# A two-layer graph attention kernel: transposes by 64-row halves, column products by 64x64 tiles, maps in the score tile

## The chip, the cores and the metric

The kernel runs on one NeuronCore of a Trainium2 chip. The core has five engines with queues of their own: TensorE (PE; its weight loads are listed apart as PEld), VectorE (DVE), ScalarE (ACT), GpSimd (POOL) and SyncE (SP), which here only starts transfers. TensorE writes its results to PSUM, where VectorE and ScalarE read them; a tile there has two banks of 512 fp32 numbers on each of 128 partitions. The metric is the device time of one execution in microseconds (us). Before the change it is 1046.4 us, the median of 14 runs (1036.08 to 1050.53).

## What is computed

Eight graphs of 2048 nodes with 64 features share one adjacency matrix. A first attention layer has four heads; keys, queries and values are all the projected nodes `h`. A second layer has one head, and two layer norms follow.

```python
def _gat_layer(h, mask, b):
    scores = jnp.einsum('...nd,...md->...nm', h, h)
    scores = jnp.where(mask, scores, NEG)
    attn = jax.nn.softmax(scores, axis=-1)
    return jnp.einsum('...nm,...md->...nd', attn, h) + b
...
    mask = graph + jnp.eye(N, dtype=graph.dtype) > 0
    h = jnp.einsum('bnc,hdc->bhnd', x, Wh)
    out_h = _gat_layer(h, mask[None, None], bh[None, :, None, :])
    cat = jnp.transpose(out_h, (0, 2, 1, 3)).reshape(B, N, H * D)
    z = jax.nn.leaky_relu(cat, negative_slope=0.2)
    h2 = jnp.einsum('bnk,dk->bnd', z, Wo)
    out2 = _gat_layer(h2, mask[None], bo)
    z2 = jax.nn.leaky_relu(out2, negative_slope=0.2)
    ...
    out = (z2 - mu) * jax.lax.rsqrt(var + LN_EPS) * gamma + beta
    return out
x = _layernorm(x + _L0_gnn_ref(x, adj, ...), axis=-1)
```

The adjacency is sparse, and denser towards the first nodes: the chance of an edge falls with the indices of both its ends.

## The kernel before

The kernel does not compute all 2048 by 2048 scores. The first 56 nodes ("hub") attend to all nodes. The other 1992 are dealt into 166 sets of 12 nodes. For each set the kernel makes a list of at most 128 nodes that any of the 12 is linked to, and works on these alone. A row of the tables in memory holds one node of all eight graphs: four pairs of graphs (index `q`, Q = 4), each pair 128 features (`p` = 0 or 1 within it) with a one on either side for the sums.

The order on every engine's queue is the order in which the code calls the operations. Waits between engines are put in by the framework, tile by tile. A PSUM tile with one buffer is written anew only when all its readers are done, and accesses of two engines to one bank are kept apart.

**Hub stage** (0 to about 150 us). The adjacency is loaded and packed, the lists of the first sets are picked on VectorE (max and match_replace), `turn_x` (L580) transposes the nodes into `xT`, and the hub's scores and values are made.

**Layer one, the sets** (about 156 to 620 us). Two sets make a group, 83 groups (NG). The loop at L1017 is pipelined: in round `i` it works on several groups at different steps. In the order of the code, TensorE does

- scores of group i+1 (`scores`, L814): 32 products of 64x64 tiles over 48 columns into tile `s` (tag S), each in two passes for fp32, so 64 in the profile. Row halves are the two graphs of a pair, and each writes its own bank;
- project of group i-1 (L525): 8 products of 64x64 over 96 columns into tile `cat` (tag C);
- values of group i (L837): 16 products of 128x64 over 65 columns into `o` (tag O);
- maps of group i-2 (`second_maps`, L873): 4 products of 128x64 over 96 columns, into columns 384 to 479 of the first bank of `cat`;
- rows of group i-3 (`second_rows`, L889): one transpose of 128x96 into the second bank of `cat`;
- columns of group i+4 (`columns`, L802): 2 products of 128x128 over 192 columns into both banks of `cat`. Their stationary operand `gram` holds a 64x64 matrix for each head twice, on its diagonal blocks, with zeros in the other two;
- the first turn of group i+3 (`turn`, L509): 4 transposes of 128x128 of gathered rows into the first bank of `t` (tag T);
- the turned values of group i (`turn_values`, L859): 4 transposes of 112x128 into `o`;
- the second turn of group i+3: 4 transposes into the second bank of `t`.

VectorE takes the mask from the scores (`weigh`, L824), inverts the sums and scales the values (`invert`, L848: two reciprocals and a product into `osb`), applies the leaky slope (`leak`), copies the maps (`keep_own`, L882, into `own`), adds the bias to the rows (`keep_rows`, L892, into `rowt`) and in the rounds that have them picks more lists (`some`). ScalarE adds the head bias (`leaky`, L514), copies the turned rows to `xTg` (L1030), takes the exponential (`lift`, L831), copies the columns to `y` (`keep_columns`, L808) and the turned values to `otb` (`keep_values`, L865). GpSimd starts the gathers of group i+5 (`gather`, L790: two indirect transfers into a ring of ten row tiles), gathers the sets' own nodes (`own_rows`, L795, every second round), copies `own`, and in the early rounds packs adjacency pieces (`more`). SP stores the rows of `keep_rows` to `table2`, and from round 30 moves the nodes for the last norm.

**Layer two** (about 625 to 1040 us). Four sets make a step, 42 steps. `turn2` (L1314) transposes the gathered rows of four sets with `turn`, 16 transposes into two `t2` tiles, which ScalarE copies to `xTg` (L1320). `scores2` (L1126) reads these as its moving operand. ScalarE's exponential, transposes of the scores (`turn_scores`, L1140), VectorE's masking (`keep_scores`, L1147, into `es`), `values2` (L1157) and the norms follow.

The names that the change touches: `turn` and its three callers (`turn_x`, the loop, `turn2`); `own_rows`, `columns` and `keep_columns`; `scores` and `scores2`, which read what was turned; `values`, `invert`, `turned`, `turn_values`, `keep_values`; `second_rows` and `keep_rows`; and the loop itself.

## Time and profile before

| | before |
|---|---|
| median of 14 runs | 1046.4 us |
| profiled execution, its own time | 1045.82 us |
| span in the profile, first to last instruction | 1043.9 us |
| mean granted TensorE clock | 0.924 |
| TensorE busy | 80% of the span |
| VectorE, ScalarE, GpSimd busy | 59%, 50%, 44% |
| transposes of layer-one and layer-two rows (L512) | 1328, 201.1 us busy |
| column products (L806) | 320, 65.4 us busy |
| turned values (L863) | 332, 45.9 us busy |
| transposes of rows for table2 (L890) | 83, 26.6 us busy |

"Busy" counts the time in which at least one instruction of the group runs. Records of TensorE overlap, since its instructions are pipelined: the mean length of one L512 is 284 ns, but four that follow each other take 0.44 us from the first to the start of what comes next. The chain of work that ended last is followed back from the last instruction: at each step to what released it, or to the instruction before it on its engine. Idle time is put down to the instruction whose end came last among those waited for. fp32 products are listed in two passes, so the counts of plain products are twice the code's; transposes run in one.

### The profile page before, as it was taken

The page shows a single profiled execution, that of the slowest core. Times are in us where ns is not written, and L with a number is a line of the kernel's source. Part 1 is how long each engine was busy: PE and PEld are TensorE (multiplying, and loading weights), DVE is VectorE, ACT ScalarE, POOL GpSimd, SP SyncE. Part 2 cuts the span into 40 slices and gives each one's busy share as a digit, 9 for nine tenths or more (in the row PEclk, how much of TensorE's full clock was granted, in tenths as well). Part 3 has the DMA queues.
Part 4 walks back from the last instruction along what each step waited for, and adds up shares of the span by engine and source line. Part 5 has one row for each costly group of instructions (what it writes and reads, how often), then busy time and mean ns, then how long its engine had stood idle before and what let it go on. Part 6 is the DMA issues. An engine that isn't in the chain of part 4 may idle for free.

```text
span 1043.9 us, 42066 instructions
## 1 busy us (share of the span) xinstructions
PE 838.6 (80%) x18437; PEld 706.5 (68%) x18437; DVE 613.3 (59%) x1369; ACT 517.5 (50%) x961; POOL 462.2 (44%) x612
## 2 busy tenths in 40 slices
PE   2976778899999999999999983677787777778740
PEld 2654567778899888888888963466666656666640
DVE  3359735688777777555555553024455555556695
ACT  2323335455666666666666651344444454545541
POOL 5542224463444556555565505344434353535400
PEclk9999889999999999999999995699889898989975
DMA  8885413453444555555555406455555565556521
GB/s 176 236 233 149 139 35 106 135 134 94 105 115 115 144 154 147 156 145 157 157 150 154 125 24 175 134 158 141 147 154 161 152 173 158 155 157 160 163 59 32
DMA packets 81794, 145.22 MB, mean 139 GB/s; under 512 B 30146, under 2 KB 46466, under 8 KB 81602
## 3 DMA queue, kind: packets, MB, share of 16 engines
q0 software_dynamic: 26720, 88.55, 31.7%
q1 hardware_dynamic: 37842, 49.65, 16.4%
q10 hardware_dynamic: 17040, 4.25, 2.2%
q8 instruction: 147, 2.41, 1.0%
q14 instruction: 45, 0.37, 0.1%
HBM read 123.91 MB, written 18.48 MB: 136 GB/s over the span
## 4 chain that ended last, share of the span: by engine, by line
PE 68%; DVE 10%; issue 7%; ACT 6%; DMA 4%; another core or an unknown queue 3%; POOL 1%; SPq 0%; ACTq 0%; DVEq 0%; POOLq 0%
PE t L512 15%; PE s L821 10%; PE o L846 8%; PE cat L806 5%; PE s L1133 5%; PE o L1165 3%; PE cat L531 3%; PE o L863 3%; PE cat L880 3%; ACT xTg L1320 3%; PE sh L1277 2%; PE e L1144 2%; PE cat L890 2%; PE oh L608 1%
## 5 line engine op out<-in xcount | busy, mean ns | idle before, releaser
L792 POOL DMA_INDIRECT g<-table,index x332 | 329.4, 992 | 411.0 <-PE o L846 173.7
L512 PE MATMUL t<-ident,g 128*128 128x128 f32 x1328 | 201.1, 284 | 24.4 <-DMA g<-table,index 12.3
L512 PEld LDWEIGHTS t<-ident,g 128*128 128x128 f32 x1328 | 160.8, 146 | 41.9 <-issue 33.8
L1320 ACT COPY xTg<-t 128x1024 f32<-128x1024 f32 x83 | 80.4, 1015 | 133.5 <-PE t L512 89.2
L826 DVE TENSOR_TENSOR e<-s,mask 128x768 f32<-128x768 f32 x83 | 79.5, 957 | 105.0 <-PE s L821 104.6
L821 PE MATMUL s<-y,xTg 64*64 64x48 f32 x5312 | 114.9, 222 | 5.2 <-issue 4.7
L821 PEld LDWEIGHTS s<-y,xTg 64*64 64x64 f32 x5312 | 98.6, 134 | 25.1 <-issue 16.4
L1152 DVE TENSOR_TENSOR es<-e,linked 128x384 f32<-128x384 f32 (+1 forms) x42 | 23.1, 551 | 141.3 <-PE t L512 94.3
L518 ACT ACTIVATE z<-cat,bhp 128x192 f32<-128x192 f32 x166 | 60.7, 417 | 85.6 <-PE cat L531 85.6
L846 PE MATMUL o<-g,e 128*64 128x65 f32 x2656 | 97.4, 227 | 0.0
L846 PEld LDWEIGHTS o<-g,e 128*64 128x64 f32 x2656 | 85.7, 140 | 9.9 <-issue 0.2
L1133 PE MATMUL s<-xTg,bd 128*32 128x128 f32 x1328 | 66.0, 314 | 29.6 <-issue 21.1
L1030 ACT COPY xTg<-t 128x1024 f32<-128x1024 f32 x83 | 84.0, 1012 | 1.9 <-PE t L512 1.9
L833 ACT ACTIVATE e<-e,shifts 128x768 f32<-128x768 f32 x83 | 79.2, 954 | 2.1 <-DVE e L826 2.0
L1133 PEld LDWEIGHTS s<-xTg,bd 128*32 128x32 f32 x1328 | 43.7, 124 | 47.6 <-issue 39.8
L812 ACT COPY y<-cat 128x384 f32<-128x384 f32 (+1 forms) x80 | 40.7, 508 | 66.2 <-DVE rowt L894 46.3
L597 ACT ACTIVATE e<-e,shifts 128x896 f32<-128x896 f32 x32 | 33.4, 1042 | 77.8 <-DVE e L594 68.4
L806 PE MATMUL cat<-xo,gram 128*128 128x192 f32 (+1 forms) x320 | 65.4, 327 | 0.0
L680 POOL TENSOR_SCALAR a<-raw 120x1024 bf16<-120x1024 int32 (+1 forms) x34 | 38.1, 1124 | 58.4 <-DMA raw<-in_adj_dram 32.6
L1165 PE MATMUL o<-g,es 128*32 128x65 f32 x2656 | 57.2, 242 | 7.1 <-DVE y_s L1188 5.1
L853 DVE RECIPROCAL rall<-o 64x8 f32<-64x8 f32 x166 | 34.1, 205 | 45.2 <-PE o L846 43.7
L854 DVE TENSOR_TENSOR osb<-o,rall 128x512 f32<-128x512 f32 x83 | 57.4, 691 | 2.9
(177 smaller groups left out, 1449.3 us busy)
## 6 DMA issues: line engine op xcount, KB each, us to landing
raw<-in_adj_dram SPq DMA_DIRECT2D x32, 480.0 KB
table<-xb SPq DMA_DIRECT2D x22, 256.0 KB
xr_s<-table SPq DMA_DIRECT2D x21, 256.0 KB
g<-table,index POOLq DMA_INDIRECT x332
table<-x SPq DMA_DIRECT2D x16, 260.0 KB
x<-in_x_dram ACTq DMA_DIRECT2D x32, 128.0 KB
table<-rowt SPq DMA_DIRECT2D x166, 24.4 KB
xb<-in_x_dram SPq DMA_DIRECT2D x164, 24.0 KB
```

Source lines behind the costliest of these rows:

```text
L512: nc.tensor.transpose(tp[:, q * P:(q + 1) * P], rows[:, q, 1:1 + P], ident)
L518: nc.scalar.activation(z[:, hp], cat[:, :, hp * n:(hp + 1) * n], AF.Identity, bias=bhp[:, hp:hp + 1], scale=1.0)
L792: nc.gpsimd.indirect_dma_start(out=t.rearrange("n q c -> n (q c)"), out_offset=None, in_=table, in_offset=bass.IndirectOffsetOnAxis(ap=ind ...
L806: nc.tensor.matmul(cat[:, k, 2 * GM:2 * GM + n], gram[:, g % 2 * 2 + k, :], held["x", g // 2][:, :n], start=True, stop=True)
L821: nc.tensor.matmul(sp[half(r), p, (q * 2 + j) * M:(q * 2 + j + 1) * M], xt[half(p), j, q, half(r)], y[half(p), (j * Q + q) * M:(j * Q + q ...
L826: nc.vector.tensor_tensor(e[:, :16 * M].rearrange("p (a q n) -> p a q n", a=2, q=Q), sp[:, :, :8 * M].rearrange("p a (q n) -> p a q n", q= ...
L833: nc.scalar.activation(e[:, :16 * M], e[:, :16 * M], AF.Exp, bias=shifts[:, 0:1], scale=1.0)
L846: nc.tensor.matmul(op[half(p), j, o0:o0 + K1], e[:, c0:c0 + 64], rw[j][:, q, sums(p)], start=True, stop=True)
L1030: nc.scalar.copy(t, held.pop(("tp", i + 2)))
L1133: nc.tensor.matmul(sp[q * 32:(q + 1) * 32, k, :], bd[u % 3][:, k, q, :], xt[:, s % 2, q, :], start=True, stop=True, tile_position=(0, q * 32))
L1165: nc.tensor.matmul(op[t * 32:(t + 1) * 32, f, k * W2 + p:k * W2 + p + K1], e[:, 2 * q + p, k, :], rw[:, q, sums(p)], start=(a == 0 and k = ...
L1320: nc.scalar.copy(t, tp)
```

## The change

Transposes are split by rows. `turn` makes two transposes for each 128x128 block: rows 0 to 63 into the first bank of the tile, rows 64 to 127 into the second, with 64 columns each. A group's second set (`j` = 1) goes beside the first within each bank. `turned_rows` gives readers the view (bank, set, pair, column). `turn_values` and `second_rows` are split in the same way, and `invert` lays its result out so that each half has its 48 rows together.

The columns are four 64x64 products for each head, two row halves by two column halves, so that the zero blocks of `gram` are not used. Each row half writes one bank, and both column halves. For this the operand `xo` has its second half with the two partition halves exchanged: `own_rows` makes three copies for one. `keep_columns` and `scores` read the result accordingly.

The maps go to columns 384 to 479 of the score tile `s` and no longer to `cat`; the rows stay in `cat`, 64 columns in each bank. In the loop the copy to `xTg` stands ahead of project; maps, columns, rows and their copies stand right behind the gathers, ahead of `leak`, the adjacency pieces and the picks; the copy of the columns stands ahead of those of maps and rows; and both turns come ahead of the turned values. One job of the hub (`slow.pop`) moves to the head of the round. In `scores2` the moving operand has two pieces of 64 columns.

```diff
@@ -508,6 +508,12 @@
-    def turn(tp, rows):
+    def turn(tp, rows, j=0):
         for q in range(Q):
-            nc.tensor.transpose(tp[:, q * P:(q + 1) * P], rows[:, q, 1:1 + P], ident)
+            c0 = (j * Q + q) * 64
+            for r in range(2):
+                nc.tensor.transpose(tp[:, r, c0:c0 + 64], rows[half(r), q, 1:1 + P], ident[half(r), half(r)])
+    def turned_rows(t):
+        return t.rearrange("c r (j q n) -> c r j q n", j=2, q=Q)
@@ -581,4 +587,5 @@
         tp = two(f"px{i}")
-        turn(tp[:, 0, :], xrow[i])
-        nc.scalar.copy(xT[:, :, i * P:(i + 1) * P], tp[:, 0, :].rearrange("c (q n) -> c q n", q=Q))
+        turn(tp, xrow[i])
+        nc.scalar.copy(xT[:, :, i * P:(i + 1) * P].rearrange("c q (r n) -> c r q n", r=2),
+                       tp[:, :, :Q * 64].rearrange("c r (q n) -> c r q n", q=Q))
@@ -796,6 +803,9 @@
-        w = min(4, NS - 4 * m)
         t = held["x", m] = work.tile([P, 2 * GM], F32, tag="xo", name=f"xo{m}", bufs=2)
-        src = xT[:, :, HUB:].rearrange("c q (k s) -> c s q k", s=NS)[:, 4 * m:4 * m + w]
-        nc.gpsimd.tensor_copy(t[:, :w * 48].rearrange("c (s q k) -> c s q k", s=w, q=Q), src)
+        v = t.rearrange("c (b s q k) -> c b s q k", b=2, s=2, q=Q)
+        src = xT[:, :, HUB:].rearrange("c q (k s) -> c s q k", s=NS)
+        nc.gpsimd.tensor_copy(v[:, 0], src[:, 4 * m:4 * m + 2])
+        b0 = min(4 * m + 2, NS - 2)
+        for r in range(2):
+            nc.gpsimd.tensor_copy(v[half(r), 1], src[half(1 - r), b0:b0 + 2])
@@ -803,15 +813,19 @@
-        n = min(4, NS - 4 * (g // 2)) * 48
+        t = held["x", g // 2]
         for k in range(2):
-            nc.tensor.matmul(cat[:, k, 2 * GM:2 * GM + n], gram[:, g % 2 * 2 + k, :], held["x", g // 2][:, :n], start=True, stop=True)
+            for r in range(2):
+                for p in range(2):
+                    nc.tensor.matmul(cat[half(p), r, (2 + k) * GM:(3 + k) * GM], gram[half(r), g % 2 * 2 + k, half(r)],
+                                     t[half(r), (p ^ r) * GM:((p ^ r) + 1) * GM], start=True, stop=True)
     def keep_columns(g, cat):
-        n = min(4, NS - 4 * (g // 2)) * 48
         if g % 2 == 0:
             held["y", g // 2] = work.tile([P, 2 * GM, H], F32, tag="yg", name=f"y{g // 2}", bufs=2)
-        nc.scalar.copy(held["y", g // 2][:, :n, g % 2 * 2:g % 2 * 2 + 2], cat[:, :, 2 * GM:2 * GM + n].rearrange("p a n -> p n a"))
+        h0 = g % 2 * 2
+        nc.scalar.copy(held["y", g // 2].rearrange("p (b n) h -> p b h n", b=2)[:, :, h0:h0 + 2, :],
+                       cat[:, :, 2 * GM:4 * GM].rearrange("p b (k n) -> p b k n", k=2))
     def scores(g, sp):
-        xt = held.pop(("T", 1, g)).rearrange("c j (q n) -> c j q n", q=Q)
-        y = held["y", g // 2][:, g % 2 * GM:(g % 2 + 1) * GM, :].rearrange("p n h -> p (n h)")
+        xt = turned_rows(held.pop(("T", 1, g)))
+        y = held["y", g // 2].rearrange("p n h -> p (n h)")
         for j in range(2):
@@ -819,5 +833,6 @@
                 for p in range(2):
+                    c0 = ((g % 2) ^ p) * GM * H + (j * Q + q) * M
                     for r in range(2):
-                        nc.tensor.matmul(sp[half(r), p, (q * 2 + j) * M:(q * 2 + j + 1) * M], xt[half(p), j, q, half(r)],
-                                         y[half(p), (j * Q + q) * M:(j * Q + q + 1) * M], start=True, stop=True)
+                        nc.tensor.matmul(sp[half(r), p, (q * 2 + j) * M:(q * 2 + j + 1) * M], xt[half(p), r, j, q, :],
+                                         y[half(p), c0:c0 + M], start=True, stop=True)
@@ -834,3 +849,3 @@
-    OQ = 256
+    OW = D + 2
@@ -843,3 +858,3 @@
                     c0 = (p * 8 + q * 2 + j) * M
-                    o0 = q // 2 * OQ + q % 2 * (D + 2) + p
+                    o0 = q * OW + p
@@ -848,11 +863,11 @@
     def invert(g, op):
-        v = op.rearrange("a j (k c) -> a (j k) c", k=2)[:, :, :2 * (D + 2)].rearrange("a w (s c) -> a w s c", s=2)
-        osb = held["o", g] = work.tile([P, 4, 2, D], F32, tag="osb", name=f"osb{g}")
-        r = rall[:, g, :].rearrange("a (w s) -> a w s", w=4)
+        v = op[:, :, :Q * OW].rearrange("a j (q c) -> a j q c", q=Q)
+        osb = held["o", g] = work.tile([P, 2, Q, D], F32, tag="osb", name=f"osb{g}")
+        r = rall[:, g, :].rearrange("a (j q) -> a j q", j=2)
         for p in range(2):
             nc.vector.reciprocal(r[half(p)], v[half(p), :, :, p * K1])
-        nc.vector.tensor_tensor(osb, v[:, :, :, 1:K1], r.unsqueeze(3).to_broadcast([P, 4, 2, D]), OP.mult)
+        nc.vector.tensor_tensor(osb, v[:, :, :, 1:K1], r.unsqueeze(3).to_broadcast([P, 2, Q, D]), OP.mult)
     def turned(op):
-        return op.rearrange("a j (k c) -> a (j k) c", k=2)[:, :, 2 * (D + 2):2 * (D + 2) + 112]
+        return op[:, :, Q * OW:Q * OW + 4 * M]
@@ -860,5 +875,8 @@
-        osb = held.pop(("o", g))
+        osb = held.pop(("o", g)).rearrange("a j q c -> a (j q c)")
         for w in range(4):
-            nc.tensor.transpose(turned(op)[:, w, :], osb[:112, w].rearrange("a s c -> a (s c)"), ident[:112, :112])
+            for p in range(2):
+                mine = slice(p * 64, p * 64 + M)
+                nc.tensor.transpose(turned(op)[:, p, w * M:(w + 1) * M], osb[mine, w * P:(w + 1) * P],
+                                    ident[mine, mine])
@@ -867,6 +885,3 @@
         ot = held["ot", g] = work.tile([P, H, GM], F32, tag="ot", name=f"otb{g}")
-        v = turned(op)
-        for p in range(2):
-            nc.scalar.copy(ot.rearrange("c h (p w n) -> c p h w n", p=2, w=4)[:, p],
-                           v[:, :, p * 64:p * 64 + M].rearrange("c w (n h) -> c h w n", h=H))
+        nc.scalar.copy(ot.rearrange("c h (p m) -> c p m h", p=2), turned(op).rearrange("c p (m h) -> c p m h", h=H))
@@ -889,3 +904,5 @@
     def second_rows(g, pr):
-        nc.tensor.transpose(pr, held.pop(("own", g)), ident)
+        t = held.pop(("own", g))
+        for r in range(2):
+            nc.tensor.transpose(pr[:, r, :], t[half(r)], ident[half(r), half(r)])
@@ -893,3 +910,3 @@
         r = rowts[g % 4]
-        nc.vector.tensor_tensor(r[:GM, 1:1 + P], pr, bob[:GM].rearrange("n p d -> n (p d)"), OP.add)
+        nc.vector.tensor_tensor(r[:GM, 1:1 + P].rearrange("n (p d) -> n p d", p=2), pr, bob[:GM], OP.add)
         dst = table2[HUB:, :].rearrange("(n s) (q c) -> s q n c", s=NS, q=Q)
@@ -1017,8 +1034,11 @@
     for i in range(-4, NG + 3):
+        if i >= 1 and slow and len(slow) % 3:
+            slow.pop(0)()
+        sp = one(f"s{i + 1}", "S")
         if 0 <= i + 1 < NG:
-            sp = one(f"s{i + 1}", "S")
             scores(i + 1, sp)
             weigh(i + 1, sp)
-        if i >= 1 and slow and len(slow) % 3:
-            slow.pop(0)()
+        if 0 <= i + 2 < NG:
+            t = held["T", 1, i + 2] = work.tile([P, 2, 512], F32, tag="xTg", name=f"xTg{i + 2}", bufs=3)
+            nc.scalar.copy(t, held.pop(("tp", i + 2)))
         cat = one(f"cat{i}", "C")
@@ -1027,5 +1047,2 @@
             held["z", i - 1] = leaky(cat, GM, f"z{i - 1}")
-        if 0 <= i + 2 < NG:
-            t = held["T", 1, i + 2] = work.tile([P, 2, 512], F32, tag="xTg", name=f"xTg{i + 2}", bufs=3)
-            nc.scalar.copy(t, held.pop(("tp", i + 2)))
         if 0 <= i + 1 < NG:
@@ -1043,2 +1060,14 @@
             (add_beta if i % 2 else load_own)((i - 30) // 2)
+        if 0 <= i - 2 < NG:
+            second_maps(i - 2, sp[:, 0, 384:384 + GM])
+        if 0 <= i + 4 < NG + NG % 2:
+            columns(i + 4, cat)
+        if 0 <= i - 3 < NG:
+            second_rows(i - 3, cat[:GM, :, 384:448])
+        if 0 <= i + 4 < NG + NG % 2:
+            keep_columns(i + 4, cat)
+        if 0 <= i - 2 < NG:
+            keep_own(i - 2, sp[:, 0, 384:384 + GM])
+        if 0 <= i - 3 < NG:
+            keep_rows(i - 3, cat[:GM, :, 384:448])
         if 0 <= i - 1 < NG:
@@ -1059,13 +1088,2 @@
             assert i + 1 + LOOK >= NG or 2 * (i + 1 + LOOK) + 1 < ready
-        if 0 <= i - 2 < NG:
-            second_maps(i - 2, cat[:, 0, 384:384 + GM])
-        if 0 <= i - 3 < NG:
-            second_rows(i - 3, cat[:GM, 1, 384:512])
-        if 0 <= i + 4 < NG + NG % 2:
-            columns(i + 4, cat)
-        if 0 <= i - 2 < NG:
-            keep_own(i - 2, cat[:, 0, 384:384 + GM])
-        if 0 <= i - 3 < NG:
-            keep_rows(i - 3, cat[:GM, 1, 384:512])
         for _ in range((2 if i < 22 or i % 2 else 1) if i >= 0 else 0):
@@ -1073,7 +1091,6 @@
                 some(1)
-        if 0 <= i + 4 < NG + NG % 2:
-            keep_columns(i + 4, cat)
         if 0 <= i + 3 < NG:
             tp = held["tp", i + 3] = one(f"t{i + 3}", "T")
-            turn(tp[:, 0, :], rows[1, 2 * (i + 3)])
+            for j in range(2):
+                turn(tp, rows[1, 2 * (i + 3) + j], j)
         if 0 <= i < NG:
@@ -1081,4 +1098,2 @@
             keep_values(i, op)
-        if 0 <= i + 3 < NG:
-            turn(tp[:, 1, :], rows[1, 2 * (i + 3) + 1])
     assert not picks and not pieces and not todo3 and done == NS
@@ -1130,5 +1145,5 @@
         for k, s in enumerate(sets[u]):
-            xt = held["T", 2, s // 2].rearrange("c j (q n) -> c j q n", q=Q)
+            xt = turned_rows(held["T", 2, s // 2])
             for q in range(Q):
-                nc.tensor.matmul(sp[q * 32:(q + 1) * 32, k, :], bd[u % 3][:, k, q, :], xt[:, s % 2, q, :], start=True, stop=True,
+                nc.tensor.matmul(sp[q * 32:(q + 1) * 32, k, :], bd[u % 3][:, k, q, :], xt[:, :, s % 2, q, :], start=True, stop=True,
                                  tile_position=(0, q * 32))
@@ -1317,3 +1332,3 @@
             for j in range(2):
-                turn(tp[:, j, :], rows[2, 2 * g + j])
+                turn(tp, rows[2, 2 * g + j], j)
             t = held["T", 2, g] = late.tile([P, 2, 512], F32, tag="xTg", name=f"xTg2_{g}", bufs=6)
```

## The prediction

> **What bounds the kernel now.** I read the page's busy table and its chain that ended last first, to see which engine sets the end.
>
> ```profile
> PE   838.6 (80%) x18437; PEld 706.5 (68%) x18437; DVE 613.3 (59%) x1369; ACT 517.5 (50%) x961; POOL 462.2 (44%) x612
> PE 68%; DVE 10%; issue 7%; ACT 6%; DMA 4%; another core or an unknown queue 3%; POOL 1%; SPq 0%; ACTq 0%; DVEq 0%; POOLq 0%
> ```
>
> TensorE holds 68% of the chain, and the line with the largest share of it, 15%, is L512, the transposes of `turn`. The work of layer one is a loop of 83 groups (one group per round) from about 156 to 620 us. Next I read the chain inside one round of it (start, us, what):
>
> ```profile
> 448.69 1.35 PE s L821 x57
> 450.05 0.39 PE cat L531 x16
> 450.44 1.08 PE o L846 x32
> 451.52 0.33 PE cat L880 x8
> 451.85 0.24 PE cat L890
> 452.10 0.65 PE cat L806 x4
> 452.75 0.44 PE t L512 x4
> 453.19 0.39 PE o L863 x4
> 453.57 0.44 PE t L512 x4
> ```
>
> There is nothing but TensorE in it: scores, project, values, maps, rows, columns, one turn, the turned values, the other turn. The next scores follow at 454.01, so a round is 5.32 us. Windows say the same: from 345 to 600 us TensorE is busy 250.1 of 255 us at a granted clock of 1.00, VectorE 154.5, ScalarE 163.6, GpSimd 144.6. A shorter TensorE stage is therefore a shorter round, until another chain takes over. The rival chain shows itself at the loop's end, where no turns and no columns are left (timeline: start, us, engine, line):
>
> ```profile
> 611.86 0.50 PE L880 MATMUL cat<-z,woT 128*64 128x96 f32 x8
> 612.08 0.42 DVE L853 RECIPROCAL rall<-o 64x8 f32<-64x8 f32 x2 [0.45 <-PE o L846]
> 612.54 0.69 DVE L854 TENSOR_TENSOR osb<-o,rall 128x512 f32<-128x512 f32 x1
> 613.28 0.60 PE L863 MATMUL o<-ident,osb 112*128 112x112 f32 x4 [0.68 <-DVE osb L854]
> 613.61 0.25 DVE L885 COPY own<-cat 128x96 f32<-128x96 f32 x1
> ```
>
> The turned values can start no sooner than 1.42 us after the first map (613.28 - 611.86): VectorE must first invert. That is the floor under the round.
>
> **The price of a half transpose.** No instruction of the trace is a 64-row transpose beside another, so I bound one pair (both halves, 64 columns each). Below: the moving columns halve, so half of L512's 0.44/4 = 0.109 us, 0.055. Side by side in other shapes: L821 runs four 64x64 products over two banks, 64 in 1.08 us, 0.067 for four; L846 two 128x64 products, 32 in 1.08, also 0.067 a pair. Above: the one row of this very shape, L505, runs in one row half alone, early, next to the first full transposes:
>
> ```profile
> 22.31 1.11 PE L505 MATMUL po<-ident,wos 64*128 64x64 f32 x4
> 24.15 1.12 PE L512 MATMUL px<-ident,x 128*128 128x128 f32 x4 [0.73 <-DVE woT L506]
> ```
>
> Four of 64 rows and 64 columns took as long as four of 128 by 128. So a half may cost a whole: 0.109 a pair if the halves overlap, 0.218 if they don't. L505 is a plain product, though, and plain products pay more for their weights: a load of 128 columns lasts 202 ns at L806 and 146 at L512. I take 0.067, by L821, the only row in which the two row halves run at once into two banks; both ends stay for the range.
>
> [...]
>
> **The change, part by part, for one round.** Columns: 8 products 64x64 over 96 columns instead of 2 of 128x128 over 192. L531 is exactly that many of that shape: 0.39 for 0.65, -0.26. Rows: one pair, 0.07 for 0.24, -0.17. Two turns: 2 x 4 pairs x 0.067 = 0.54 for 0.88, -0.34. Turned values: 4 pairs, 0.27 for 0.39, -0.12. One more change of tile form (64x64 between the 128x64 maps and the 64x128 transposes): the first load of L821 after the turns waits 0.17 us for "issue" where loads within a stage wait for none, +0.17. Sum: -0.72, so 4.60 a round.
>
> [...]
>
> What hides the rest. *VectorE's invert:* before the turned values TensorE now has maps 0.33, the change 0.17, columns 0.39, rows 0.07 and both turns 0.54 = 1.50 us of cover against 1.42, just enough; without it each missing us is a us of the round. *Maps in the score tile:* the next scores wait for the copy of `own` (L885, 0.25), now right behind the invert: 1.42 + 0.27 = 1.69 after the first map, against TensorE's 1.50 + 0.27 + 0.17 = 1.94. The maps wait for `weigh` to have read the tile; it begins about when scores end and lasts 0.96, project and values cover 1.47. *VectorE's queue:* keep_rows now stands behind ScalarE's copy of the columns (before, that copy waited for keep_rows); queued behind it are leak, the list picks and the next `weigh`. VectorE is busy 65.7 of 85 us between 260 and 345 (16.2 rounds of 5.24): 4.05 a round, which fits into 4.6, but little is left. *ScalarE:* the xTg copy (1.01) goes ahead of leaky (0.73); 163.6 busy of 255 us is 3.4 a round of 5.3; keep_values is one copy for two. *GpSimd:* own_rows is three copies for one (0.53 each two rounds), some 0.3 more in two rounds, and the copy of `own` moves past the adjacency pieces; it is 57% busy, no gather waits behind it that TensorE needs within two rounds. *SP:* the row stores (1.25 a round) only move ahead.
>
> Rounds: 61 from 260 us on at -0.72 = -44; the 19 between 156 and 260, of which many last 7 to 9 us for hub work, key products and VectorE, at half: -7; the last three nothing. Loop: -51.
>
> Layer two: 16 transposes a step of four sets, 42 steps, 1.74 us before and 16 pairs x 0.067 = 1.07 after: -0.67 a step, -28 if all of it is on the path. But the chain there reads (817 to 821 us)
>
> ```profile
> 817.40 0.33 PE t L512 x3
> 817.73 0.07 issue
> 817.79 0.64 PE t L512 x4
> 818.43 0.10 issue
> 818.53 2.45 PE t L512 x9
> ```
>
> and nine transposes need 0.98 us, not 2.45: the copy that follows is released some 1.5 us after the work, by something no view names. I count half, -14. Layer two's other edit, one moving operand in two pieces, has the shape of L880's and costs nothing there. The hub stage transposes 16 tiles beside idle TensorE: 0.
>
> Sum against the profiled execution's own 1045.8 (span 1043.9, 1.9 around it; the median is 0.6 higher): 1045.8 - 51 - 14 = **981**.
>
> **Rivals.**
> *Late release.* The turned values now come last, with only scores (1.08) between them and project, which needs their copy; before, a turn stood there too. At 513 us L863's last record ends at 513.06 and its copy runs 514.11 to 514.65: 1.6 later. If that lag is TensorE's and stays, project waits 1.6 - 1.08 - 0.17 = 0.35: 61 x 0.35 + 19 x 0.17 = 24 given back, **1005**. For it: the copy was idle 0.48 for L512. Against: 0.5 of the lag was the copy of the columns on ScalarE, which moves earlier. 20%.
> *Halves cost wholes, overlapped (0.109).* 13 pairs x 0.042 = 0.55 lost, 0.17 a round left: 61 x 0.17 + 2 = 12, layer two 0: **1034**. L505 speaks for it. 14%.
> *Halves don't overlap (0.218).* 13 x 0.151 = 1.96, so +1.24 a round, 83 x 1.24 = 103, and 42 x (3.49 - 1.74) = 73 in layer two: **1222**. With 70 full rounds and half of layer two, 70 x (13p - 1.59) + 21 x (16p - 1.74) = 0 at p = 0.119: above that price of a pair the change loses. For it: L505; against: L821's two banks. With milder prices just above that point, 16%.
> *Does nothing that can be told* (within 0.5%, 5 us, about what a measurement of this kernel can tell from no change): half the pairs' gain eaten by VectorE where lists are picked and by more changes of form. 6%.
>
> **How the numbers follow.** The forecast has 44%. Faster: 44 + 20 + 14 = 78%, same 6%, slower 16%. Its own lower end: pairs at 0.055 (13 x 0.012 x 70 = 11, and 8 in layer two), layer two in full (14), early rounds in full (7): 981 - 40 = 941. Upwards the range takes in the late release and the overlapped wholes, to 1040; left out are the slower case and part of "same".
>
> **What would show it.** In the trace after: pairs of L514 about 0.067 apart, columns near 0.39, rounds of 4.6 us, TensorE still with nearly all of the chain. Wrong if L514's eight take over 0.4 us, if project waits for `otb` or scores for `own`, or if VectorE's share of the chain in the loop grows past a fifth; in layer two if steps stay at 9 us though L514 is shorter.

## The result and the profile after

The changed kernel takes 1163.4 us (median of 10 runs) where the one before takes 1046.7 (47 runs): a ratio of 1.1115, 95% interval 1.1082 to 1.1147. It is slower by 11%, and the forecast of 981 has the wrong sign. The profiled execution has a span of 1160.6 us and a mean granted clock of 0.871 (0.924 before). The experiments below were timed in five sessions, each with its own runs of the kernel before. In two of them that kernel took 877 and 880 us, in the other three 1040 to 1044, so every run is compared only with the kernel before of its own session. Executions over 1.5% above the fastest of their kernel in a session are left out of the ratios (one of the changed kernel's, one of the last order version's), so a ratio can differ a little from that of the medians.

The busy table and the chain that ended last, page of after:

```profile
PE   838.9 (72%) x21252; PEld 685.9 (59%) x21252; DVE 612.7 (53%) x1369; ACT 559.4 (48%) x878; POOL 485.0 (42%) x696
PE 46%; DVE 15%; ACT 12%; issue 11%; another core or an unknown queue 8%; DMA 4%; POOL 2%; SPq 1%; DVEq 0%; POOLq 0%; ACTq 0%
```

TensorE is busy as long as before (838.6), in 2815 more matrix instructions, but its share of the chain fell from 68% to 46%, and ScalarE's doubled. Where the 117 us went, from the first scores, values and second-layer products of both traces: the loop of layer one took 464.3 and takes 557.8 (start of the first scores to start of the last values), the way from there to the first scores of layer two 34.3 and 49.8, layer two to its last values 357.8 and 361.9; the loop starts 3.4 later, and the tail is the same. So 93 of 117 us lie in the loop, 15 at the entrance of layer two.

One round of the loop, by the chain of waits of after (start, us, what); its first products ran at half clock, of which more below:

```profile
561.41 0.92 PE cat L537 x16
562.33 1.93 PE o L861 x32
564.26 0.64 PE s L895 x8
564.90 0.49 PE cat L818 x16
565.39 0.19 PE cat L907 x2
565.58 0.49 PE t L514 x16
566.08 0.23 PE o L880 x7
...
567.18 0.23 ACT y L825
567.41 0.43 issue
567.84 0.90 ACT otb L886
```

Both turns take 0.49 (8 pairs, 0.061 each), columns 0.49, rows 0.19, turned values 0.23: as short as forecast or nearly so. But the chain now leaves TensorE. Project (L537) waits for `otb`, `otb` stands behind `y` on ScalarE, and `y` starts at 567.18, though the rows, whose report it waits for, end at 565.58 in the records (the view below names L880, whose record ends later). A report is here the change of TensorE's semaphore that lets a waiting engine go on. Timelines of this stretch, first after, then before (start, us, engine, line, form, idle time and what ended it):

```profile
564.34 0.97 POOL L799 DMA_INDIRECT g<-table,index  x1 [0.41 <-PE o L861]
...
565.61 0.95 POOL L799 DMA_INDIRECT g<-table,index  x1 [0.30 <-issue]
...
567.18 0.88 ACT L825 COPY y<-cat 128x384 f32<-128x384 f32 x1 [3.23 <-PE o L880]
...
568.79 0.31 PE L537 MATMUL cat<-otb,whT 64*64 64x96 f32 x4 [0.50 <-ACT otb L886]
```

```profile
447.64 1.04 POOL L792 DMA_INDIRECT g<-table,index  x1 [0.30 <-issue]
...
448.32 0.52 ACT L812 COPY y<-cat 128x384 f32<-128x384 f32 x1 [0.69 <-DVE rowt L894]
...
449.28 0.54 ACT L870 COPY otb<-o 128x192 f32<-128x192 f32 x2 [0.45 <-PE t L512]
```

The trace also holds the moments of these reports. Set beside the records' ends they show what no view names: while GpSimd issues the round's two gathers, TensorE's reports come late, and they come together some 0.6 us after the second gather's end. After: rows end 565.58, report 567.16; turned values 566.62 and 567.39; the gathers end at 566.56. Before: turned values 448.25 and 449.20, second turn 448.69 and 449.26; the gathers end at 448.68. Reports of scores, project and values, outside the gathers, follow within 0.1. For the rows of after the lag is 1.6 us here; in the rounds from 300 to 600 us it is 1.5 in the median and 2.5 at most.

The gathers start when the values are done (their ring slot comes free), so this fixes a second chain in every round: project 0.56, values 1.08, 0.1 to the gathers, 2.9 from their start to the reports, then whatever stands between the reports and project. Before that is the `otb` copy, 449.20 to project at 449.88, 0.7: 5.3 us, as long as the round, and so it did not show. After it is `y` and `otb` in a row, 567.16 to 568.79, 1.6: 6.2 us. The rounds of after from 300 to 600 us have a median of 6.35. In 41 of 45 of them project starts within 0.08 us of the end of `otb`; in before in 33 of 55, and in before without gathers (next section) in 7 of 59.

In addition TensorE now idles ahead of project (12.8 us from 345 to 600, 12.0 of them for `otb`; it is busy 206.8 of these 255 us, where it was 250.1), and in some rounds its granted clock is half. Windows of after during the values of two neighbouring rounds (stretch, its length, busy time and count of PE, PEld, DVE, ACT and POOL, granted clock, DMA share, GB/s):

```profile
562.30:564.20 1.90, 1.90 (x38) 1.90 (x36) 0.04 (x1) 1.55 (x3) 0.95 (x3) 0.50 0.10 25
569.40:570.40 1.00, 1.00 (x36) 1.00 (x38) 0.31 (x1) 1.00 (x4) 0.00 (x0) 1.00 0.25 68
```

At 0.50 the values take 1.93 for 1.08, and such a round 7.4 for 6.3. Over 345 to 600 us the clock is 0.95 where it was 1.00: seven stretches at half clock in some 40 rounds, most of them 3.4 us long.

### The profile page after: what moved, and what is told of

Read it like the earlier page. It is cut to its first block, busy times and chain, and to the rows that moved or that the text cites. A ratio compares the mean times of both kernels' runs of the same rounds, so it can differ in the third digit from the quotient of the medians.

```text
span 1160.6 us, 47545 instructions
## 1 busy us (share of the span) xinstructions
PE 838.9 (72%) x21252; PEld 685.9 (59%) x21252; DVE 612.7 (53%) x1369; ACT 559.4 (48%) x878; POOL 485.0 (42%) x696
## 4 chain that ended last, share of the span: by engine, by line
PE 46%; DVE 15%; ACT 12%; issue 11%; another core or an unknown queue 8%; DMA 4%; POOL 2%; SPq 1%; DVEq 0%; POOLq 0%; ACTq 0%
PE t L514 7%; PE o L861 6%; PE o L880 5%; PE s L1148 4%; PE cat L818 3%; ACT otb L886 3%; ACT y L825 3%; PE cat L537 3%; PE s L895 3%; ACT xTg L1335 3%; PE s L836 2%; PE o L1180 2%; PE sh L1292 2%; DMA raw<-in_adj_dram 2%
## 5 line engine op out<-in xcount | busy, mean ns | idle before, releaser
L514 PE MATMUL t<-ident,g 64*128 64x64 f32 x2656 | 134.1, 236 | 68.0 <-issue 49.2
L514 PEld LDWEIGHTS t<-ident,g 64*128 64x128 f32 x2656 | 109.7, 146 | 89.8 <-issue 78.9
L836 PE MATMUL s<-y,xTg 64*64 64x48 f32 x5312 | 130.8, 232 | 33.1 <-issue 31.7
L836 PEld LDWEIGHTS s<-y,xTg 64*64 64x64 f32 x5312 | 109.8, 145 | 51.3 <-issue 45.7
L825 ACT COPY y<-cat 128x384 f32<-128x384 f32 x80 | 68.8, 859 | 145.7 <-PE o L880 112.3
L861 PE MATMUL o<-g,e 128*64 128x65 f32 x2656 | 108.3, 241 | 0.6 <-issue 0.6
L911 DVE TENSOR_TENSOR rowt<-cat,bob 96x128 f32<-96x128 f32 x83 | 24.0, 289 | 152.5 <-ACT y L825 150.4
L886 ACT COPY otb<-o 128x384 f32<-128x384 f32 x83 | 72.3, 871 | 42.2 <-PE o L880 20.8
L810 POOL COPY xo<-xT 64x96 f32<-64x96 f32 x84 | 29.2, 348 | 119.1 <-DMA g<-table,index 113.6
L537 PE MATMUL cat<-otb,whT 64*64 64x96 f32 x1328 | 52.4, 278 | 23.8 <-ACT otb L886 21.8
```

The lines of the kernel that those rows point to most:

```text
L514: nc.tensor.transpose(tp[:, r, c0:c0 + 64], rows[half(r), q, 1:1 + P], ident[half(r), half(r)])
L537: nc.tensor.matmul(cat[half(j), s, hp * n:(hp + 1) * n], whT[half(s), h * D:(h + 1) * D], ot[half(s), h, :], start=True, stop=True)
L825: nc.scalar.copy(held["y", g // 2].rearrange("p (b n) h -> p b h n", b=2)[:, :, h0:h0 + 2, :], cat[:, :, 2 * GM:4 * GM].rearrange("p b (k ...
L836: nc.tensor.matmul(sp[half(r), p, (q * 2 + j) * M:(q * 2 + j + 1) * M], xt[half(p), r, j, q, :], y[half(p), c0:c0 + M], start=True, stop=True)
L861: nc.tensor.matmul(op[half(p), j, o0:o0 + K1], e[:, c0:c0 + 64], rw[j][:, q, sums(p)], start=True, stop=True)
L886: nc.scalar.copy(ot.rearrange("c h (p m) -> c p m h", p=2), turned(op).rearrange("c p (m h) -> c p m h", h=H))
```

## The experiments

Times are medians beside the kernel before of the same session. "Held" is said of reports that come late during gathers as above. "Loop", "entrance" and "layer two" are the three stretches defined above, from each profiled execution (before: 464.3, 34.3, 357.8; after: 557.8, 49.8, 361.9).

### Without GpSimd's gathers in layer one

```diff
+        if layer == 1:
+            nc.sync.dma_start(out=t.rearrange("n q c -> n (q c)"), in_=table[s % 8 * P:(s % 8 + 1) * P, :])
+            return
         nc.gpsimd.indirect_dma_start(...)
```

The changed kernel:

> The changed kernel, but layer one's gathers on GpSimd (L799) are replaced by plain loads of 128 rows in a row, issued by SyncE: the same bytes land in the same tiles. The neighbours' values are therefore wrong; so that no sum vanishes, the exponents of layer one's and layer two's lists are flattened (scale 0.01), which costs the same instructions. Theory A (in the changed kernel TensorE's results are reported late while GpSimd issues a gather: rows L907 end at 565.58 in the records, their update comes at 567.16, 0.60 after the second gather's end, and ScalarE's two copies and then project follow from there): rounds fall from 6.3 and 7.4 to 4.6 to 5.0 us, the updates follow the records within 0.1, layer one's loop takes 380 to 430 us instead of 561, the run about 980 to 1030. Theory B (the half transposes themselves finish later than their records show): the late updates stay, rounds stay over 6, the run over 1120.

The kernel before:

> The kernel before with the same replacement (plain loads by SyncE for layer one's gathers, flattened exponents). Theory A: the updates after L863 and L512 (0.85 and 0.65 late in the rounds from 345 to 600) follow the records within 0.1; the round stays near 5.3, since TensorE's own work fills it, so the loop stays at 440 to 468 and the run at 1015 to 1045. Theory B: L512's updates stay over 0.5 late. Theory C (the loop before was bound by the landing of rows and not by TensorE): rounds under 5.0.

Measured (one timed run each, before 1044.3): 1070.0 for the changed kernel, over the 980 to 1030 expected, and 1015.6 for the other. These versions compute wrong values, so they are no faster kernels. All reports follow the records within 0.2 in layer one, in both. In most rounds of the kernel before scores follow scores after 5.00 us, and its loop is 22 us shorter (442.6). Chain of waits of that run:

```profile
400.87 1.08 PE s L824 x64
...
405.87 1.08 PE s L824 x64
```

So TensorE's own round was 5.00, not 5.32, and the rest was scores that took 1.35 for 1.08 during the hold. The changed kernel's undisturbed round, by the chain of waits of its run:

```profile
453.26 1.08 PE o L864 x32
...
455.36 0.49 PE t L514 x16
455.85 0.24 PE o L883 x8
456.09 1.08 PE s L839 x64
457.17 0.48 PE cat L537 x16
457.65 0.20 PE o L864
```

From values to values 4.39 us, all TensorE: 0.61 less than 5.00, where the forecast had 0.72 less. Theory B falls. Of the 93 us that the change loses in the loop, 63 are gone without the gathers; but 30 stay: the rounds average 5.46 and the loop takes 472.9 beside 442.6. The trace of instruction transfers points at a cause for these. TensorE's instructions come in packets of 16 KB, one for every 254 that it runs (169 in the whole run of after, 22 more than before for 5630 instructions more, 256 each). Of its 88 stalls over 0.25 us between 180 and 590 us 50, 47.5 us in all, end 1.05 to 1.55 us after such a packet has landed; with a packet every 4.3 us some 10 would fall there by chance. The kernel before (with gathers) has 3 such stalls (3.4 us). The changed one with its gathers has 30 (18.8 us), but of 195, so that some 19 may be chance. If the supply is the cause, a round of 324 instructions in 4.4 us outruns it at times, where 274 in 5.3 do not; that is the author's reading of the timing, and no run changes the supply alone.

### The two copies on ScalarE

```diff
-        nc.scalar.copy(ot.rearrange("c h (p m) -> c p m h", p=2), turned(op).rearrange("c p (m h) -> c p m h", h=H))
+        nc.scalar.copy(ot.rearrange("c h (p m) -> c p h m", p=2), turned(op).rearrange("c p (m h) -> c p h m", h=H))
```

and `y` likewise, head innermost in place of node.

> The changed kernel with ScalarE's copies of the columns (L825, 0.86) and of the turned values (L886, 0.87) walking their elements in another order (innermost index contiguous where it is written); the same data. Theory A: both copies stand one behind the other between the late update and project (0.66 and 0.90 of a round of 6.28), and each would take some 0.52 as before: 0.66 to 0.7 less a round, 82 rounds, 1163 to about 1105, and more if TensorE's clock then no longer falls to half in every second round. If the copies are covered: 1163. If the price is not one of the order of elements: 1163 and L825 still 0.86.

Measured: 1139.1, 1.0936 (1.0897 to 1.0976). The group of the `y` copy (line, form, count, busy us, mean ns, idle before it) in the changed kernel, then in this one:

```profile
L825 ACT COPY y<-cat 128x384 f32<-128x384 f32 x80 | 68.8, 859 | 145.7 <-PE o L880 112.3 <-PE cat L907 19.2 <-remote 11.0
```

```profile
L825 ACT COPY y<-cat 128x384 f32<-128x384 f32 x80 | 40.9, 511 | 121.8 <-PE o L880 77.9 <-PE cat L907 26.5 <-remote 13.9
```

The `otb` copies took 871 and take 481. The order of elements alone made the two copies 0.35 and 0.39 dearer. The dear orders write 16 bytes and more apart; the order of the reads changes with that of the writes, and no run parts the two. Of the 58 us expected 20 came (loop 537.3), and the round only went from 6.35 to 6.30. In 21 of 47 rounds GpSimd starts its gathers 0.5 us and more after the values, and scores stall during them (those at 470.68 take 3.20 us for 1.08). Project now starts within 0.08 of the end of `otb` in 9 of 47 rounds alone: TensorE itself, stalled in scores, is as late as the copies. So the chain over `y` and `otb` is not the only path that the hold lengthens.

### The halves of the transposes, alone and undone

Layer two alone in halves, on the kernel before (`turn2` with the two-half transposes, `scores2` reading two pieces):

> The kernel before with the transposes of layer two alone in two halves of 64 rows (32 for 16 a step, and the scores' moving operand in two pieces); layer one untouched. Forecast's own reason: 14 to 28 us faster, 1020 to 1032. Theory A (layer two's steps wait for late updates during the gathers, not for the transposes): within 6 us of 1046. Theory B (halves really cost more than wholes): layer two, 358 us long, gets longer by 20 or more, 1066 and up.

Measured: 1069.0, 1.0251 (1.0218 to 1.0284): entrance 50.3, layer two 364.6. The halves cost 25 us there, and 16 of them at the entrance, where GpSimd issues 24 gathers in a row for 30 us. With on-time reports the entrance cost is gone but not the other (see the gathers one group later, below). In after one `t2` tile's transposes end at 747.12 and are reported at 752.70.

Layer one alone in halves, in two sessions:

> The kernel before with the turns of layer one alone in two halves of 64 rows (16 transposes for 8 a round), order, columns, rows, turned values and layer two untouched. By the pair price of 0.060 in the changed kernel's records TensorE saves 8 x (0.109 - 0.060) = 0.39 a round. Theory A1 (while GpSimd issues a gather only the reports of TensorE's results are withheld, it works on meanwhile): rounds between 5.0 (the round with plain loads) and 5.34, the run 1020 to 1046. Theory A2 (while GpSimd issues a gather TensorE gets through only so many instructions, whatever their size): 8 more instructions a round in that window cost more than 0.39, rounds of 5.5 and more, the run over 1055.

> Again the kernel before with the turns of layer one alone in halves, for a chip with held reports (on one without, it took 1.0071 of the time before, at rounds of 5.05: each of the two turns 0.39 for 0.44, the turned values between them 0.53 for 0.39, because the form of the tiles changes twice). With held reports: A1 1035 to 1055, A2 over 1065. Without: again 1.005 to 1.009.

Measured: 882.6 beside 877.1 (1.0071, 1.0047 to 1.0095) in a session in which the reports of transposes were on time in both layers (median 0.02, all turns within 0.1), and 1041.8 beside 1039.6 (1.0021, 0.9997 to 1.0046) in one in which they were held. The first shows why TensorE gained nothing, chain of waits of that run:

```profile
505.87 0.39 PE t L518 x6
506.26 0.53 PE o L869 x4
506.79 0.39 PE t L518 x8
```

A turn is 0.39 for 0.44, and the whole turned values between two turns of halves 0.53 for 0.39: two changes of tile form cost more (0.14) than the halves of two turns save (0.10). In the held session the loop is 464.3, as in the profiled execution of before.

The changed kernel with whole transposes of gathered rows in both layers, and the changed kernel again in the same session:

> The changed kernel with the transposes of gathered rows whole again in both layers (128x128, 8 for 16 a round, 16 for 32 a step), everything else as changed: order, columns, rows, turned values, maps in the score tile, dear copies. Theory A2 (during a gather TensorE gets through few instructions): on a chip with held reports layer two and the way into it win back the 25 us that the halves alone cost there, and the loop part of its 93: 1090 to 1120. Theory A1 (only the order and the copies lengthen the second chain): layer two wins 25, the loop nothing: 1135 to 1145. On a chip without held reports whole turns are 0.39 a round dearer: 15 to 35 us slower than the changed kernel beside it.

> The changed kernel, not altered. In the call before this one the kernel before took 877 us on its chip, and there TensorE's updates followed the records within 0.02 even while GpSimd gathered; on the chip of the first experiments (1044) they were held back. Theory A: the loss comes from the held reports, so on a chip without them the changed kernel is not slower by 11% but near the kernel before or under it: TensorE's own round is 4.4 (seen in undisturbed rounds with plain loads), 5.0 before, so up to 0.6 x 70 = 42 us and some 10 of layer two less, 825 to 880 beside 877. On a chip with held reports: 1150 to 1175 beside 1044. Theory B (the change is slower in itself): over 900 beside 877.

Measured: 1122.8 beside 1154.1 for the changed kernel and 1039.6 for before. The entrance and layer two win back 24 (38.9 and 346.2 for 49.6 and 359.2), the loop 6. That session held the reports back again, so the question that the second expectation put, what the changed kernel does where they are not held, was not answered.

### The columns alone

```diff
+                    nc.tensor.matmul(cat[half(p), r, (2 + k) * GM:(3 + k) * GM], gram[half(r), g % 2 * 2 + k, half(r)],
+                                     t[half(r), (p ^ r) * GM:((p ^ r) + 1) * GM], start=True, stop=True)
```

> The kernel before with the columns' products alone as 8 products of 64x64 (and the half swapped operand: three GpSimd copies for one in every second round), their copy written in the cheap order of elements; order, turns, rows and turned values untouched. TensorE saves 0.26 a round by its rows. Theory A1: rounds 5.05 to 5.34, the run 1022 to 1046. Theory A2: the columns run ahead of the held window or at its start (L806 was reported on time in most rounds), so little is lost: 1022 to 1050. If GpSimd's extra copies delay the gathers: over 1055.

> Again the kernel before with the columns alone in 64x64 tiles and the cheap copy, for the case that reports are held back (without that, it took 1.034 of the time before, since GpSimd's half-swapped copies wait in every second round for gathers just issued, and columns for them). By that wait alone: 1.02 to 1.04 again. If small products among gathers cost by their number as well: 1.05 and more.

Measured: 909.0 beside 877.1 (1.0344) and 909.6 beside 880.2 (1.0309), both in sessions without held reports. Many rounds are 5.2 to 6.5 where the others are 4.98: by the chain of waits GpSimd's two half-swapped copies wait for the landing of the gathers issued just ahead of them, and the columns for them. The same wait stands in the changed kernel:

```profile
L810 POOL COPY xo<-xT 64x96 f32<-64x96 f32 x84 | 29.2, 348 | 119.1 <-DMA g<-table,index 113.6
```

There, with longer rounds, it lies beside others: with `own_rows` moved ahead of the gathers

> The changed kernel with own_rows ahead of the gathers in GpSimd's queue, nothing else. On a chip with held reports the wait of L810 lies beside others (columns wait for it 0.2 us in all): within 8 of the changed kernel's 1155 to 1163. If GpSimd's wait carries the loss: 1120 or less. On a chip without held reports, where the kernel before with the small columns had every second round at 5.4 to 6.4 behind this very wait: 20 to 40 us under the changed kernel.

it took 1152.1 beside 1039.8, 1.1061 (1.0991 to 1.1131), loop 556.1: nothing, though the idle time of L810 for the gathers fell from 113.6 to 53.6 us.

### The order of the work

The gathers one group later and behind the copy of `own`, on both kernels:

> The kernel before with layer one's gathers one group later (LOOK 4 instead of 5, with the same ten buffers, so that a gather no longer waits for this round's values) and issued behind the copy of own, so that they start near the turned values and lie over scores and project. Theory A1: the turned values are reported on time and the late reports fall on the scores, which have a round of slack: rounds 5.0 to 5.2, the run 1020 to 1040. Theory A2: the scores, 64 products, now lie in the window: rounds over 5.5, the run over 1055. If the rows then land too late for the turns: TensorE waits for gathered rows, over 1060.

> The changed kernel with the two ScalarE copies in the cheap order of elements (that alone: 1139) and the gathers one group later and behind the copy of own, as in the run beside it. Theory A1: rows and turned values are reported on time, rounds 4.6 to 5.2, the run 1040 to 1080. Theory A2: what the gathers cost moves from the turns to the scores, rounds stay over 6, 1120 to 1145.

Measured: 956.9 and 983.5 beside 877.1. Both miss: the rows land too late for the turns (idle before L512 47.7 us for the gathers, before L514 82.8). In both runs the reports of rows, turns and turned values were on time (medians of 0.02). Yet the scores, which now fall into the gathers, are reported late here too: in the kernel before 0.26 us in the median and 0.86 at most, in the changed one up to 1.5. So the sessions of 877 and 880 us have a smaller hold, not none; where this text says "without held reports" it means the reports that a round of that version waits for. They also give the only view of layer two in halves with on-time reports: entrance 31 us beside 30, layer two 232 beside 225.

The order alone, added to the kernel before and taken out of the changed one:

> The kernel before with the changed kernel's order of the loop alone (maps in the score tile, columns ahead of rows and their copy first, both turns ahead of the turned values, the copy xTg ahead of leaky), every product and transpose in its old shape. Of the loop's loss of 93 us the dear copies explain 20 and the halved turns 6. Theory A1, the order carries most of the rest (the report that the columns' copy waits for, and the one that the turned values' copy waits for, both fall behind the gathers, the two copies stand one behind the other ahead of project): rounds 5.8 to 6.3, the run 1080 to 1110 beside 1044; on a chip without held reports 885 to 900 beside 877. Rival, the smaller shapes are needed for the loss: 1044 to 1060.

> The changed kernel with the order of the loop of before (rows ahead of columns, their copy behind keep_rows, a turn on each side of the turned values, leaky ahead of xTg); all shapes, the dear copies, the maps in the score tile and layer two as changed. Theory A1: the loop wins back 40 to 60 of its 93: 1100 to 1125 beside 1044, and TensorE's clock rises from 0.87. Rival: within 15 of 1160. On a chip without held reports: 850 to 890 beside 877.

Measured: 1068.4, 1.0266 (1.0211 to 1.0322), and 1152.7, 1.1077 (1.1013 to 1.1141). So the order is not what carries the loss: with the old shapes most rounds are 5.05 to 5.6, and the old order with the new shapes has a median of 6.59. But with the old shapes it costs 28 us of its own. Seven rounds between 368 and 450 us take 6.7 to 7.2, and there the chain of waits runs over VectorE: `leak` (L523) takes 1.7 to 2.1 us for 0.55 in 20 of 54 rounds, where it stands beside GpSimd's additions for the last norm (L928). Timeline of one of them:

```profile
402.86 2.05 DVE L523 SCALAR_TENSOR_TENSOR z<-z 128x384 f32<-128x384 f32 x1
403.20 1.29 POOL L928 TENSOR_TENSOR xb<-xb,bet 128x512 f32<-128x512 f32 x1
```

The chain of waits of the second, the end of one round:

```profile
516.47 0.70 PE t L514 x8
517.16 0.03 issue
517.19 0.30 DVE rowt L911
...
517.51 0.51 ACT y L825
518.02 0.14 issue
518.16 0.90 ACT otb L886
```

Here `rowt`, `y` and `otb` all stand behind the held report of 517.16, 1.94 to the next project at 519.10: 0.56 + 1.08 + 0.1 + 2.9 + 1.94 = 6.6, as measured. What differs from the old shapes is which report is held. Medians from 300 to 600 us, runs with held reports, of products issued since the first gather's start against the report's time after that start:

| products | report after | what it is |
|---|---|---|
| 5 | 1.08 | columns, before |
| 5 | 1.30 | rows, before with the new order |
| 13 | 2.84 | turned values, before |
| 17 | 2.92 | second turn, before |
| 18 | 2.85 | rows, after |
| 18 | 2.79 | columns, after with the old order |
| 25 | 2.96 | second turn, before with halves |
| 42 | 3.07 | turned values, after |

The first few products' reports slip through at once, the rest wait for the end of the gathers, however many or short they are. Time since the start does not sort them: the transpose into `pb`, which comes twice in the loop, is reported within 0.02 where it is the first product of the hold (before, 0.8 after the start) and 1.8 and 1.9 late where it is the 19th (after, at 1.11). With the whole column products (2, listed as 4) the report for `y` slips through, and `y` is copied during the hold; with the small ones (8, listed as 16) it does not, and its copy joins the chain. That reading rests on these traces; no run changed the number of products alone among held reports.

A version with the old order, the cheap copies, whole transposes in layer two and `own_rows` ahead of the gathers:

> As the run before it, with the two copies in the cheap order of elements, whole transposes in layer two alone, and GpSimd's own_rows ahead of the gathers instead of behind them (its half-swapped copies L810 waited 113.6 us in all for the landing of gathers issued just ahead). Theory A1: the second chain project, values, gathers, late report, copy, project is 5.0 to 5.1, TensorE's own round 4.3 to 4.6: rounds 5.0 to 5.2 beside 5.4, layer two as before: 1020 to 1040 beside 1044. On a chip without held reports rounds of 4.4 to 4.8: 825 to 860 beside 877. If it is over the time before, a cause is still missing.

Measured: 1101.4, 1.0539 (1.0453 to 1.0624), where 1020 to 1040 was expected; the profiled execution of 1104.6 has a loop of 522.7 and rounds of 6.08. Layer two is back; the loop is not, since `rowt`, `y` and `otb` still wait for the held report (1.26 ahead of project, for 5.9 by the sum above), and since the gathers, behind `own_rows`, start 0.56 after the values in half of the rounds.

### The number of instructions

> The kernel before with 16 idle products of 64x64 over 4 columns behind the maps of every round (64 more TensorE instructions for some 274, about as the changed kernel has; output columns nobody reads). By the scores' row, 32 products in 1.08, they are some 0.54 of work. Theory A2 (what costs is the number of instructions: TensorE is fed 16 KB of them, some 254, at a time, and stalls for the next lot, and during gathers it gets through few): more than their work, rounds of 6.1 and up, the run over 1100. By their work alone: rounds of 5.8 to 5.9, the run 1075 to 1090, like the run beside it.

> The control: the kernel before with 2 idle products of 128x128 over 128 columns behind the maps of every round (8 more TensorE instructions, some 0.5 of work by the columns' row, 2 of 192 columns in 0.65). Both theories: rounds of 5.8 to 5.9, the run 1075 to 1090.

Measured: 922.5 (1.0481, 1.0418 to 1.0545) and 907.7 (1.0288, 1.0238 to 1.0339) beside 880.2, in a session without held reports. The usual rounds are 5.57 and 5.50, so each costs about its work; the loops are 481.5 and 470.2, and 0.07 x 82 = 6 of that difference lies in the usual rounds. At most the other 5 are the price of the number. Where reports are not held the number costs little; where they are, this was not measured.

## Why the prediction was wrong

*TensorE bounds the loop, so a shorter stage is a shorter round.* This is the step that failed. The views did show nothing but TensorE in the round, but a second chain of 5.3 us (project, values, gathers, late report, `otb`) was as long, so that shortening TensorE's work between values and scores could win little. What the runs show in its place: without gathers the change takes TensorE's round from 5.00 to 4.39, with them the round goes from 5.34 to 6.35, since the reports come only after the gathers. The sign of it stood in the chain that the prediction quotes: scores took 1.35 there, with nothing named that kept them, and 1.08 elsewhere.

*The prices.* Pairs of halves 0.067, measured 0.061; columns 0.39, measured 0.49; rows 0.07, measured 0.19; turned values 0.27, measured 0.24. The change of tile form was priced at 0.17, and two of them cost 0.14 in the turned values of the layer-one split. The saving by these was 0.72 a round; without the gathers it was 0.61. TensorE's side of the sum nearly held.

*The covers.* VectorE's invert and the copy of `own` were hidden as said. ScalarE's "one copy for two" was not: the new orders of elements made two copies 0.7 dearer together, 20 us by the run that undid it, and the forecast put no price on them. *GpSimd: own_rows some 0.3 more in two rounds* missed its wait for gathers in flight; undoing half of it won nothing here, and by the chain of waits it is what made the columns alone 3% slower where the rounds are short.

*Rivals.* Late release came nearest: it named the turned values, the lag and project's wait. It priced the lag at what one round showed less the work that follows, 24 us, and let it stay as it was; it is a window tied to the gathers, it took in the report for `y` as well, and it made the run slower and not merely less fast. Halves that cost as wholes, overlapped or not, did not happen.

*Layer two, -14.* The prediction saw that a copy was released 1.5 us late "by something no view names" and then counted half the gain. It was the same hold (in before the reports of L512 come 2.0 us late in the median of layer two), and there more and smaller transposes cost 25 us; with on-time reports they were still 7 us slower and not 14 to 28 faster.

The sum for after, as far as the runs carry it: entrance and layer two some 20 to 25 (halves). Of the 93 in the loop 63 hang on the gathers, by the two runs without them; the other 30 are laid to the supply of instructions by its timing alone. Single changes took back 20 (orders of elements) and 6 (halved turns). The sum of 6.2 a round for 5.3, over 82 rounds, would put 74 on `y` and `otb` behind the held report, dear copies included, and the half clock adds to it; but cheaper copies won back a third of what that sum promised, so how the loss divides between these copies and TensorE's own stalls in scores stays open.

*Open:* why TensorE's reports are held at all during gathers, and why so much less in two of the five sessions (there layer two of the kernel before's variants takes 224 us for 358). It is not the chip alone: the record has chip number 14 for one of these two and for one of the other three. What the changed kernel takes in such a session was not measured; its version with later gathers took 983.5 beside 956.9 for the kernel before with the same. Why only the first few products slip through is open too. No version here that computes the result beat the kernel before.

## What to carry to other kernels

An engine that holds nearly all of the chain may hide a second chain just under it: work out the longest loop that leaves that engine, by what releases what, before a shorter stage is counted as a shorter round. Where a copy starts well after the records of what it waits for, find the event at which the report came, and ask what ran then; here the report came 2.8 to 3.1 us after the first gather's start, behind 13 products as behind 42. And a rewritten layout has to be priced at its readers and copies, element order included.

## What had not been expected of the hardware

- TensorE's reports were held while GpSimd issued indirect gathers: up to 2.5 us in the loop, where they were let go about 0.6 after the second gather, and 5.6 at the entrance of layer two, in the midst of 24 gathers. Plain loads of the same bytes held nothing (0.2 at most). In sessions with a smaller hold the kernel before took 877 for 1044.
- TensorE seems, by the timing alone, to have run out of instructions: at 4.4 us a round 50 of 88 stalls (47.5 us) ended 1.05 to 1.55 us after a 16 KB packet of them had landed.
- With TensorE busy 206.8 of the 255 us from 345 to 600 (250.1 before), some rounds ran at a granted clock of 0.50: seven stretches of 3.4 us, one of them double, and none there in the kernel before.
- The same 384 elements a partition took ScalarE 0.86 or 0.51 us by the order in which they were walked.
- VectorE's `leak` took 1.7 to 2.1 us instead of 0.55 beside GpSimd's additions of 128x512 numbers.
